# A 5x5 convolution by pairs of rows with shared products, laid into a selective scan

## The chip, the cores and the metric

The kernel runs on one core of a Trainium2 chip. The core has five engines that work side by side: TensorE (PE in the profile, with its weight loads listed as PEld), VectorE (DVE), ScalarE (ACT), GpSimd (POOL) and the queue of SyncE (SP), which here issues the transfers. Each engine takes its instructions strictly in the order of its queue. The metric is the time of one execution in microseconds of device time, the median of several runs. All data are 32-bit floats.

## The reference, cut to what matters

The input x is 4 images of 128 channels and 64 x 64 points. Four layers follow each other, each of the form x = x + f(group_norm(x)) with 32 groups:

```
layer 0: full self-attention over the 4096 points
layer 1: 5x5 convolution, 128 -> 128 channels, padding 2; its taps are
         built from two small tables, an index table and an identity
layer 2: 1x1 projection, split into 2 x 64 channels, the second half
         reversed in time; per half a 4-tap convolution, SiLU, softplus,
         then a selective scan with 64 states per channel over 4096 steps
         (h = exp(delta*A) h + delta*x*B, y = C h + D x); 1x1 projection back
layer 3: 3x3 convolution with bias (the offsets it also computes do not
         reach the output: where(m > 0.01, out, out))
```

The change concerns layer 1:

```
xp = pad(gn(x), 2)
y[o, r, c] = sum over channels i and taps (dy, dx) of
             w[o, i, dy, dx] * xp[i, r + dy, c + dx]
```

## The kernel before, in words

The 128 channels lie on the 128 partitions; an image is 4096 columns. A product on PE is a 128 x 128 weight times 512 columns, accumulated into one PSUM bank (512 floats per partition).

The scan of layer 2 is the backbone. `scan_core` cuts it into ticks: 4 images x 4 chunks of 1024 steps x 2 directions x 16 groups of states x 2 groups of channels, 256 ticks to an image and 1024 in all. In a tick ACT makes the decays exp(delta*A) (`decay`, L801), POOL the drives delta*x*B (`drive`, L808, one 128 x 1024 multiplication), DVE the recurrence itself (`recur`, L818) and the multiplication by C (L821). In some ticks POOL takes that multiplication (`weigh`, L839): two of five for images 0 to 2, one of three for image 3. PE adds up over the states (`collect`, L853). Drives are written two ticks ahead of the recurrence into three buffers; loads of the rows go out four ticks ahead.

Everything else is written as generators that yield after each small step the time that the step is thought to take on PE (PRODUCT = 0.86 us for one 512-column product, HOP and SLOT for other steps). `images` chains them: for each image attention (L405 and L417), the 5x5 convolution (`conv`, L571, closing in `add`, L954 and L955), and the preparation of the scan (`scan_prep`, `scan_operands`), and after those of all four images the back part of images 0 to 2 (projection back, 3x3 convolution). The main loop at the end of `program` interleaves them with the scan: each tick gives a credit of PACE, in two halves, and steps of the other work are written out until the credit is used up. The order on every queue is fixed that way when the program is built; at run time nothing but semaphores decides. If half of the next image's preparation is not written when the scan of one image ends, the loop writes all of it at once (`before`). During the scan of image 3 the credit is ENDPACE.

So image 0's attention, convolution and the first half of its preparation run before any scan. Those of images 1 to 3 run between the ticks of images 0 to 2, and the back parts of images 0 to 2 between the ticks of image 3; the back part of image 3 comes last.

The convolution before: `conv` copies the normalised image into a padded buffer of 68 x 68 in four pieces (ACT, L311), and for each block of 8 rows runs 25 products, one per tap, into one of three banks. After the third product of the next block DVE adds the finished bank to x (L954) and takes the statistics of the sum for the next norm (L955).

Buffers of size: `A0` and `A1` hold a padded or plain image in turn, `V` attention's values, then the normalised input of the scan preparation, and later the padded image of the 3x3 convolution. The 25 taps `cw` are built by DVE during attention of image 0; the 9 taps of the 3x3 convolution `m3` have a buffer of their own, loaded at the start.

Of the kernel before, what the change touches and what calls it, by code (L numbers as in the profile page):

```python
# [24 lines left out]
F32 = mybir.dt.float32  # L25
I32 = mybir.dt.int32
AF = mybir.ActivationFunctionType
ALU = mybir.AluOpType
# [4 lines left out]
P = 128  # L33
GROUPS = 32
GN_EPS = 1e-5
CH = 1024
MM = 512
HALF = P // 2
PAD = 2
# [3 lines left out]

PRODUCT, HOP, SLOT, PACE, ENDPACE, AHEAD = 0.86, 1.7, 0.7, 2.9, 1.5, 4


BQ, BK, BX, BP, CONVB, BD, DSKIP, MAINB, CONVW, ALOG = 0, 1, 2, 3, 4, 5, 6, 7, 8, 12
# [3 lines left out]
def conv_preact_kernel(  # L53
# [16 lines left out]
    nc = tc.nc  # L70
    B, C, H, W = x.shape
    L = H * W
# [4 lines left out]
    NTAP = xhat.shape[1]  # L77
    HP, WP = H + 2 * PAD, W + 2 * PAD
# [8 lines left out]
    const = ctx.enter_context(tc.tile_pool(name="const", bufs=1))  # L87
    small = ctx.enter_context(tc.tile_pool(name="small", bufs=2))
    dram = ctx.enter_context(tc.tile_pool(name="dram", bufs=2, space=DRAM))
    ps = ctx.enter_context(tc.tile_pool(name="ps", bufs=1, space=PSUM))  # L90
    pools, ready = {}, set()

    def bank(tag, name):
        return pools.get(tag, ps).tile([P, MM], F32, tag=tag, name=name)
# [12 lines left out]
    nc.scalar.dma_start(wback[:, 0, :], mats[:, 4, :])  # L107
    nc.scalar.dma_start(wback[:HALF, 1, :], mats[HALF:, 4, :])
    nc.scalar.dma_start(wback[HALF:, 1, :], mats[:HALF, 4, :])
    m3 = const.tile([P, main_w.shape[1], C], F32, name="m3")  # L110
    nc.scalar.dma_start(m3, main_w)

    ident = const.tile([P, P], F32, name="ident")
    make_identity(nc, ident)
# [18 lines left out]
    for d in range(2):  # L133
        r = slice(d * HALF, (d + 1) * HALF)
# [74 lines left out]
    nc.vector.tensor_scalar(hbias, cbias, 0.5, None, ALU.mult)  # L209


    cw = const.tile([P, NTAP, C], F32, name="cw")

    def build_conv_weights(tmp):
        xx_sb = tmp.tile([P, NTAP, C], F32, name="xx_sb")
        nc.sync.dma_start(xx_sb, xhat)
        id_sb = tmp.tile([P, C], F32, name="id_sb")
        nc.sync.dma_start(id_sb, identity)
        picked = tmp.tile([P, 2, NTAP, C // 2], F32, name="picked")
        for n, (which, table, inds) in enumerate((("xx", wxx, indsxx), ("id", wid, indsid))):  # L220
            nr, oc = table.shape[1], table.shape[2]
            acc = picked[:, n]
            one = cw.rearrange("p k c -> p (k c)")[:, : NTAP * oc]
            one = one.rearrange("p (k o) -> p k o", o=oc)
            tab = tmp.tile([P, nr, oc], F32, name=f"tab{which}")
            nc.sync.dma_start(tab, table)
            ii = tmp.tile([P, NTAP], I32, name=f"ii{which}")
            nc.sync.dma_start(ii, inds.to_broadcast([P, NTAP]))
            fi = tmp.tile([P, NTAP], F32, name=f"fi{which}")
            nc.vector.tensor_copy(fi, ii)  # L230

            ng = tmp.tile([P, NTAP], F32, name=f"ng{which}")
            nc.vector.tensor_scalar(ng, fi, 0.0, float(nr), ALU.is_lt, ALU.mult)
            nc.vector.tensor_tensor(fi, fi, ng, ALU.add)
            nc.vector.tensor_scalar(fi, fi, 0.0, float(nr - 1), ALU.max, ALU.min)
            for r in range(nr):
                hit = tmp.tile([P, NTAP], F32, name=f"hit{which}{r}")
                nc.vector.tensor_scalar(hit, fi, float(r), None, ALU.is_equal)
                hit_b = hit.unsqueeze(2).to_broadcast([P, NTAP, oc])
                tab_b = tab[:, r : r + 1, :].to_broadcast([P, NTAP, oc])  # L240
                if r == 0:
                    nc.vector.tensor_tensor(acc, tab_b, hit_b, ALU.mult)
                else:
                    nc.vector.tensor_tensor(one, tab_b, hit_b, ALU.mult)
                    nc.vector.tensor_tensor(acc, acc, one, ALU.add)
                yield HOP

        for t in range(2):
            def every(ap):
                return ap.rearrange("p k (o t) -> p k o t", t=2)[:, :, :, t]  # L250

            idb = id_sb.rearrange("p (o t) -> p o t", t=2)[:, :, t].unsqueeze(1)
            idb = idb.to_broadcast([P, NTAP, C // 2])
            nc.vector.tensor_tensor(every(xx_sb), every(xx_sb), picked[:, 0], ALU.mult)
            nc.vector.tensor_tensor(every(cw), picked[:, 1], idb, ALU.mult)
            yield HOP
        nc.vector.tensor_tensor(cw, cw, xx_sb, ALU.add)

    ASIZE, VSIZE = (H + 4) * (W + 4), (H + 2) * (W + 2)

    def large(n, name):
        return pools["big"].tile([P, ASIZE], F32, tag=f"A{n % 2}", name=name)
# [6 lines left out]
    def stats_tile(name):  # L272
        return small.tile([P, NM, 6], F32, tag=f"gn_st{name[0]}", name=f"st_{name}")
# [36 lines left out]
    def normalise(dst, src, gn):  # L310
        nc.scalar.activation(dst, src, AF.Identity, scale=gn[0], bias=gn[1])  # L311
# [230 lines left out]
    def conv(b, xs, tag, st, weights, k, finish, name, residual=False):  # L542

        pad = k // 2
        hp, wp = H + 2 * pad, W + 2 * pad
        size = VSIZE if tag == "V" else ASIZE
        xp = pools["big"].tile([P, size], F32, tag=tag, name=f"xp{name}_{b}")
        xp = xp[:, : hp * wp].rearrange("p (h w) -> p h w", w=wp)
        nc.gpsimd.memset(xp[:, :pad, :], 0.0)
        nc.gpsimd.memset(xp[:, hp - pad :, :], 0.0)  # L550
        nc.gpsimd.memset(xp[:, pad : hp - pad, :pad], 0.0)
        nc.gpsimd.memset(xp[:, pad : hp - pad, wp - pad :], 0.0)
        gn = yield from group_norm(st, f"{name}{b}")
        xh = xs.rearrange("p (h w) -> p h w", w=W)

        def piece(i):
            h0, h1 = i * H // 4, (i + 1) * H // 4
            normalise(xp[:, pad + h0 : pad + h1, pad : pad + W], xh[:, h0:h1, :], gn)

        piece(0)  # L560
        yield HOP / 2
        piece(1)
        done = None
        for i in range(NM):
            if i < 2:
                piece(2 + i)
            acc = bank("saz"[i % 3], f"pc{name}_{b}_{i}")
            for t in range(k * k):
                dy, dx = divmod(t, k)
                y = i * RPM + dy  # L570
                nc.tensor.matmul(  # L571
                    acc.rearrange("p (r w) -> p r w", w=W), weights[:, t, :],
                    xp[:, y : y + RPM, dx : dx + W],
                    start=t == 0, stop=t == k * k - 1 and not residual,
                )
                if t == 2 and done is not None:
                    finish(*done)
                if t % 3 == 2:
                    yield 3 * PRODUCT
            if residual:  # L580
                nc.tensor.matmul(acc, ident, xs[:, bass.ts(i, MM)], start=False, stop=True)
            yield PRODUCT
            done = i, acc
        yield HOP
        finish(*done)

# [334 lines left out]
    def program(safe):  # L923
        mats4, ynds, ends = {}, {}, {}
        ready.clear()

        def load(tile, b):
            for c in range(NCH):
                nc.sync.dma_start(tile[:, bass.ts(c, CH)], xf[b][:, bass.ts(c, CH)])
                yield 0.0  # L930
# [13 lines left out]
        def front(b, xn, v):  # L944

            xs = large(b + 1, f"xs_{b}")[:, :L]
            yield from load(xs, b)
            st = stats_tile(f"e{b}")
            yield from attention(b, xs, xn, v, st, safe)
            st2 = stats_tile(f"s{b}")  # L950

            def add(i, acc):
                cut = bass.ts(i, MM)
                nc.vector.tensor_tensor(xs[:, cut], acc, xs[:, cut], ALU.add)  # L954
                nc.vector.bn_stats(st2[:, i, :], xs[:, cut])  # L955

            yield from conv(b, xs, f"A{b % 2}", st, cw, 5, add, "e")

            def mat(name):
                return dram.tile([NCH, P, CH], F32, tag=name, name=f"{name}_{b}")  # L960

            mats4[b] = (
                [mat("bm"), mat("cm")], mat("dd"), mat("dxd"), mat("xcd"),
                dram.tile([P, L], F32, tag="xsd", bufs=B, name=f"xsd_{b}"),
            )
            ynds[b] = dram.tile([NM, P, MM], F32, tag="ynd", bufs=B, name=f"ynd_{b}")
            operands = yield from scan_prep(b, xs, st2, mats4[b])
            if b + 1 < B:
                return (yield from both(operands, start(b + 1, 10)))
            yield from operands  # L970
# [52 lines left out]
        inner, last = range(PER, NM - PER), range(NM - PER, NM)  # L1023
# [15 lines left out]
        with ExitStack() as es, tc.manual_schedule():  # L1039
# [60 lines left out]
            for _ in chain(end(B - 1, range(PER)), back(B - 1)):  # L1100
                pass

    program(False)


# [11 lines left out]
    with tc.If(again > 0):  # L1117
        program(True)
# [59 lines left out]
```

## Time and profile before

| what | value |
|---|---|
| time, median of 3 runs | 4684.2 us (4680.8 to 4685.3) |
| profiled span | 4679.2 us |
| PE busy | 4151.4 us, 89% |
| DVE busy | 3764.6 us, 80% |
| POOL busy | 3522.0 us, 75% |
| ACT busy | 2313.3 us, 49% |
| 5x5 convolution on PE (L571 into pce) | 1600 records, two to a product |
| scan on DVE, multiplications L821 and recurrences L818 | one or two of each to a tick |

The page shows the share of busy time of each engine, the span in 40 slices, and groups of instructions by line. A record of PE is half a product of the program, and its listed length includes the time it overlaps with its neighbours, so the count of records and their spacing say more than their mean. Shares over the whole span mix three stages with different limits; they have to be read from windows.

### The profile page before, as it was taken

How to read it: one execution, taken by the hardware profiler on the slowest of the kernel's cores; microseconds unless marked ns; L12 is line 12 of the kernel's file. 1: busy time of each engine (PE TensorE's matmuls, PEld its weight loads, DVE VectorE, ACT ScalarE, POOL GpSimd, SP SyncE). 2: the span in 40 equal slices, each digit the busy share in tenths (PEclk: the TensorE clock that was granted, in tenths of full speed). 3: DMA queues.
4: the chain of work that ended last, by engine and by line, in shares of the span. 5: the costliest groups of instructions: out<-in, count | busy, mean ns of one | idle time of the engine just before them, and what ended most of it. 6: DMA issues, size and time to landing. Idle time of an engine off the chain costs nothing. (4 is left out here: it accounts for less than half of the span.)

```text
span 4679.2 us, 43928 instructions
## 1 busy us (share of the span) xinstructions
PE 4151.4 (89%) x13840; PEld 1538.3 (33%) x13840; DVE 3764.6 (80%) x3673; ACT 2313.3 (49%) x4166; POOL 3522.0 (75%) x1644
## 2 busy tenths in 40 slices
PE   6999997999999988999999979999999748576767
PEld 3444443333333323333333323333333202121212
DVE  7222104999999998999999999899989899999993
ACT  2333205666665356666654466666543644444431
POOL 2333202898888978898989869888889689999992
PEclk9999998999999999999999989999999968787878
DMA  1000005544444555445444564454445565656561
GB/s 65 0 0 1 0 5 184 186 168 163 163 169 150 178 203 214 155 164 175 169 158 164 187 227 169 157 177 164 168 147 177 201 224 199 229 193 229 186 230 46
DMA packets 210434, 718.90 MB, mean 154 GB/s; under 512 B 24848, under 2 KB 25744, under 8 KB 210064
## 3 DMA queue, kind: packets, MB, share of 16 engines
q1 hardware_dynamic: 208448, 714.69, 43.7%
q8 instruction: 111, 1.82, 0.2%
q10 hardware_dynamic: 1744, 1.32, 0.1%
q14 instruction: 131, 1.07, 0.1%
HBM read 649.07 MB, written 66.85 MB: 153 GB/s over the span
## 5 line engine op out<-in xcount | busy, mean ns | idle before, releaser
L808 POOL TENSOR_TENSOR db<-dx,br 128x1024 f32<-128x1024 f32 x1024 | 2404.4, 2367 | 377.8 <-DVE hc L818 94.8
L801 ACT ACTIVATE da<-de,a_neg 128x512 f32<-128x512 f32 (+1 forms) x1795 | 1343.9, 752 | 926.9 <-DVE da L818 600.3
L405 PE MATMUL sc<-r,x 128*128 128x512 f32 x2048 | 1087.5, 613 | 44.0 <-ACT last L834 16.4
L417 PE MATMUL acc<-pt,v 128*128 128x512 f32 x2048 | 1049.1, 594 | 1.5
L839 POOL TENSOR_TENSOR hc<-hc,cr 128x1024 f32<-128x1024 f32 x392 | 928.5, 2369 | 19.0 <-ACT last L834 15.5
L411 ACT ACTIVATE pt<-sc 128x512 f32<-128x512 f32 x1024 | 604.0, 590 | 613.4 <-PE sc L405 577.8
L821 DVE TENSOR_TENSOR hc<-da,cr 128x512 f32<-128x512 f32 (+1 forms) x1095 | 847.1, 774 | 71.7 <-DVE da L818 0.9
L853 PE MATMUL y<-hc,sel 128*32 128x512 f32 x4096 | 654.0, 653 | 272.7 <-POOL hc L839 247.5
L818 DVE TENSOR_TENSOR_SCAN da<-da,last,db 128x512 f32<-128x512 f32 (+1 forms) x474 | 740.5, 1562 | 16.2 <-POOL db L808 8.9
L571 PE MATMUL pce<-xpe,cw 128*128 128x512 f32 x1600 | 724.6, 606 | 24.8 <-ACT xpe L311 17.8
L818 DVE TENSOR_TENSOR_SCAN da<-da,da,db 128x512 f32<-128x512 f32 x463 | 595.8, 1287 | 26.2 <-ACT da L801 25.8
L405 PEld LDWEIGHTS sc<-r,x 128*128 128x128 f32 x2048 | 358.9, 190 | 642.7 <-issue 385.9
L417 PEld LDWEIGHTS acc<-pt,v 128*128 128x128 f32 x2048 | 388.4, 190 | 498.9 <-issue 480.0
L571 PEld LDWEIGHTS pce<-xpe,cw 128*128 128x128 f32 x1600 | 297.3, 190 | 452.4 <-issue 424.0
L818 DVE TENSOR_TENSOR_SCAN hc<-da,last,db 128x512 f32<-128x512 f32 (+1 forms) x294 | 442.7, 1506 | 2.9 <-POOL db L808 1.2
L818 DVE TENSOR_TENSOR_SCAN hc<-da,hc,db 128x512 f32<-128x512 f32 x308 | 395.1, 1283 | 45.1 <-ACT da L801 15.6
L459 POOL TENSOR_TENSOR sidep<-sidep,pt 128x512 f32<-128x512 f32 x120 | 161.3, 1344 | 307.0 <-ACT pt L411 307.0
L853 PEld LDWEIGHTS y<-hc,sel 128*32 128x32 f32 x4096 | 93.5, 111 | 728.7 <-POOL hc L839 333.2
L571 PE MATMUL pcm<-xpm,m 128*128 128x512 f32 x576 | 287.5, 647 | 31.4 <-ACT xpm L311 31.4
L459 DVE TENSOR_TENSOR sided<-sided,pt 128x512 f32<-128x512 f32 x120 | 90.3, 753 | 249.7 <-ACT pt L411 248.4
L818 DVE TENSOR_TENSOR_SCAN da<-da,db 128x512 f32<-128x512 f32 (+1 forms) x158 | 235.7, 1492 | 17.0 <-ACT da L801 9.3
L834 ACT COPY last<-da 128x1 f32<-128x1 f32 x473 | 74.0, 156 | 270.1 <-DVE hc L821 268.2
(167 smaller groups left out, 2251.9 us busy)
## 6 DMA issues: line engine op xcount, KB each, us to landing
br<-bm SPq DMA_DIRECT2D x512, 512.0 KB, 5.0
cr<-cm SPq DMA_DIRECT2D x512, 512.0 KB, 3.9
de<-dd SPq DMA_DIRECT2D x64, 512.0 KB, 4.6
dx<-dxd SPq DMA_DIRECT2D x64, 512.0 KB, 6.2
x<-in_x_dram SPq DMA_DIRECT2D x16, 512.0 KB, 5.7
xs<-in_x_dram SPq DMA_DIRECT2D x16, 512.0 KB, 6.8
xsd<-xs SPq DMA_DIRECT2D x16, 512.0 KB, 5.1
xcd<-xc SPq DMA_DIRECT2D x16, 512.0 KB, 2.7
```

Of the source, the lines that this page charges most:

```text
L405: nc.tensor.matmul(sc, xn[:, bass.ts(j, P)], rq[blk], start=True, stop=True)
L411: nc.scalar.activation(pt, sc, AF.Exp)
L417: nc.tensor.matmul(acc[blk], v[:, j, :], ring[:, u % NRING, :], start=j == 0, stop=j == NJT - 1)
L459: eng.tensor_tensor(s, s, ring[:, u % NRING, :], ALU.add)
L571: nc.tensor.matmul(acc.rearrange("p (r w) -> p r w", w=W), weights[:, t, :], xp[:, y : y + RPM, dx : dx + W], start=t == 0, stop=t == k * ...
L801: nc.scalar.activation(da, rep["de", b, c, d, g][:, bass.ts(h, size)], AF.Exp, scale=a_neg[:, at(i)])
L808: nc.gpsimd.tensor_tensor(dbs[i], rep["dx", b, c, d, g], rows["b", b, c, d, q], ALU.mult)
L818: nc.vector.tensor_tensor_scan(h, da, db[:, cut], before, ALU.mult, ALU.add)
L821: nc.vector.tensor_tensor(hc[:, cut], h, rows["c", b, c, d, q][:, cut], ALU.mult)
L834: nc.scalar.copy(last[b][:, at(i)], end)
L839: nc.gpsimd.tensor_tensor(hcs[i], hcs[i], rows["c", b, c, d, q], ALU.mult)
L853: nc.tensor.matmul(y[r : r + SG, :], sel, hcs[i - KG + 1 + gg][:, bass.ts(h, MM)], start=q == 0, stop=False, tile_position=(0, r), skip_gr ...
```

## The change

Two vertically adjacent output rows share work. With x0 to x5 the six padded input rows that they see and w0 to w4 the five rows of taps (each standing for its five horizontal taps):

```
q  = (w1 + w2) x2 + (w3 + w4) x4
y0 = q + w0 x0 + w1 (x1 - x2) + w3 (x3 - x4)
y1 = q + w0 x1 + w2 (x3 - x2) + w4 (x5 - x4)
```

This takes 2 + 3 + 3 rows of taps to two rows of output in place of 5 + 5. The new `conv_pairs` works on chunks of 16 rows: one bank for q (8 rows of pairs), one for the even and one for the odd rows, 512 columns each.

- The sums of taps w1 + w2 and w3 + w4 are made once by DVE (two additions of 128 x 640) behind the 25 taps.
- The differences of neighbouring rows are made by POOL into a buffer `diffs` in `V`: per image eight subtractions of 8 or 9 rows of 66 columns, each behind the normalised piece it reads.
- ACT copies q from its bank to SBUF. In image 0 POOL adds the copy to x, once for even and once for odd rows. In the later images (`lean`) PE adds it to the banks of the even and odd rows by a product with the identity.
- DVE adds the finished banks to x with a row stride and takes the statistics after the odd rows.
- The padded buffer has rows of 66 columns; a row's right padding is the next row's left padding.
- `m3` now lies in the first nine taps of `cw`. The 3x3 taps are loaded when the last image's 5x5 convolution has been written; a copy of the 5x5 taps is kept in device memory for a second pass that runs only if attention's sums fall out of range.
- PACE goes from 2.9 to 2.8.

The core of the diff:

```diff
-PRODUCT, HOP, SLOT, PACE, ENDPACE, AHEAD = 0.86, 1.7, 0.7, 2.9, 1.5, 4
+PRODUCT, HOP, SLOT, PACE, ENDPACE, AHEAD = 0.86, 1.7, 0.7, 2.8, 1.5, 4
...
-    m3 = const.tile([P, main_w.shape[1], C], F32, name="m3")
-    nc.scalar.dma_start(m3, main_w)
...
+    m3 = cw[:, : main_w.shape[1], :]
...
+        for n in range(2):
+            row = cw[:, (1 + 2 * n) * 5 :]
+            nc.vector.tensor_tensor(
+                cw[:, NTAP + n * 5 : NTAP + (n + 1) * 5, :], row[:, :5], row[:, 5:10], ALU.add
+            )
+        nc.sync.dma_start(kept, m3)
...
+        def odd(j, n):
+            nc.gpsimd.tensor_tensor(
+                diffs[:, j * WQ : (j + n) * WQ].rearrange("p (h w) -> p h w", w=WQ),
+                rows[:, 2 * j + 1 : 2 * (j + n) : 2, :], rows[:, 2 * j + 2 : 2 * (j + n) + 1 : 2, :],
+                ALU.subtract,
+            )
...
+        for c in range(L // CH):
+            j = c * CK
+            if c < 2:
+                piece(2 + c)
+            if c < 3:
+                differences(c + 1)
+            accs = [
+                (bank("s", f"pq_{b}_{c}"), ((SUM12, image, 2 * j + 2), (SUM34, image, 2 * j + 4))),
+                (bank("a", f"pe0_{b}_{c}"),
+                 ((0, image, 2 * j), (1, diff, j), (3, diff, j + 1))),
+                (bank("z", f"pe1_{b}_{c}"),
+                 ((0, image, 2 * j + 1), (2, diff, NP + j + 1), (4, diff, NP + j + 2))),
+            ]
+            for n, (acc, parts) in enumerate(accs):
+                k, total = 0, len(parts) * K5
+                for w, view, r in parts:
+                    for dx in range(K5):
+                        k += 1
+                        nc.tensor.matmul(
+                            flat(acc), cw[:, w * K5 + dx, :], view(r, dx),
+                            start=k == 1, stop=k == total and (n == 0 or not lean),
+                        )
+                        if k == 3 and done is not None:
+                            done()
+                            done = None
+                        if k % 3 == 0:
+                            yield 3 * PRODUCT
+                if n == 0:
+                    qs = pools["bg"].tile([P, MM], F32, tag="w", bufs=4, name=f"q_{b}_{c}")
+
+                    def done(acc=acc, qs=qs, c=c):
+                        nc.scalar.copy(qs, acc)
+                        for y in range(0 if lean else 2):
+                            nc.gpsimd.tensor_tensor(
+                                chunk(xs, c, y), chunk(xs, c, y), flat(qs), ALU.add
+                            )
+                    yield PRODUCT
+                else:
+                    if lean:
+                        nc.tensor.matmul(acc, ident, qs, start=False, stop=True)
+                        yield PRODUCT
+
+                    def done(acc=acc, c=c, y=n - 1):
+                        add(c, y, acc)
...
-            yield from conv(b, xs, f"A{b % 2}", st, cw, 5, add, "e")
+            yield from conv_pairs(b, xs, f"A{b % 2}", st, st2, b > 0 or safe)
+            if b + 1 == B:
+                nc.sync.dma_start(m3, main_w)
```

More of the change, by code (lines that the diff above doesn't have):

```diff
@@ L209, in conv_preact_kernel @@
     nc.vector.tensor_scalar(hbias, cbias, 0.5, None, ALU.mult)
-    cw = const.tile([P, NTAP, C], F32, name="cw")
+    SUM12, SUM34 = 5, 6
+    cw = const.tile([P, NTAP + 10, C], F32, name="cw")
+    taps5 = cw[:, :NTAP, :]
+    m3 = cw[:, : main_w.shape[1], :]
+    kept = dram.tile([P, main_w.shape[1], C], F32, tag="kept", bufs=1, name="kept")
     def build_conv_weights(tmp):
@@ L249, in every @@
             def every(ap):
-                return ap.rearrange("p k (o t) -> p k o t", t=2)[:, :, :, t]
+                return ap.rearrange("p k (o t) -> p k o t", t=2)[:, :NTAP, :, t]
             idb = id_sb.rearrange("p (o t) -> p o t", t=2)[:, :, t].unsqueeze(1)
@@ L256, in build_conv_weights @@
             yield HOP
-        nc.vector.tensor_tensor(cw, cw, xx_sb, ALU.add)
-    ASIZE, VSIZE = (H + 4) * (W + 4), (H + 2) * (W + 2)
+        nc.vector.tensor_tensor(taps5, taps5, xx_sb, ALU.add)
+        for n in range(2):
[4 more added lines that the diff above has]
+        nc.sync.dma_start(kept, m3)
+    ASIZE, VSIZE = HP * (W + PAD) + PAD, (H + 2) * (W + 2) + PAD
     def large(n, name):
@@ L585, in conv, with conv_pairs, piece, even @@
         finish(*done)
+    def conv_pairs(b, xs, tag, st, st2, lean):
+        NP, CK = H // 2, CH // W // 2
+        WQ = W + PAD
+        xp = large(b, f"xpe_{b}")
+        rows = xp[:, : HP * WQ].rearrange("p (h w) -> p h w", w=WQ)
+        xh = xs.rearrange("p (h w) -> p h w", w=W)
+        nc.gpsimd.memset(rows[:, :PAD, :], 0.0)
+        nc.gpsimd.memset(xp[:, (HP - PAD) * WQ : HP * WQ + PAD], 0.0)
+        nc.gpsimd.memset(rows[:, PAD : HP - PAD, :PAD], 0.0)
+        gn = yield from group_norm(st, f"e{b}")
+        diffs = pools["big"].tile([P, VSIZE], F32, tag="V", name=f"df_{b}")
+        nc.gpsimd.memset(diffs[:, 2 * (NP + 1) * WQ :], 0.0)
+        def piece(i):
+            h0, h1 = i * H // 4, (i + 1) * H // 4
+            normalise(rows[:, PAD + h0 : PAD + h1, PAD:], xh[:, h0:h1, :], gn)
+        def odd(j, n):
[4 more added lines that the diff above has]
+            )
+        def even(j, n):
+            at = (NP + j) * WQ
+            nc.gpsimd.tensor_tensor(
+                diffs[:, at : at + n * WQ].rearrange("p (h w) -> p h w", w=WQ),
+                rows[:, 2 * j + 1 : 2 * (j + n) : 2, :], rows[:, 2 * j : 2 * (j + n) - 1 : 2, :],
+                ALU.subtract,
+            )
+        def differences(i):
+            last = i == 3
+            odd(8 * i, 8 + last)
+            even(8 * i + 1, 8 + last)
+        def by_rows(t, n):
+            return [t[:, o : o + n * WQ].rearrange("p (h w) -> p h w", w=WQ) for o in (0, PAD)]
+        padded, differ = by_rows(xp, HP), by_rows(diffs, 2 * (NP + 1))
+        def image(r, dx):
+            late = dx // PAD > 0
+            dx -= late * PAD
+            return padded[late][:, r : r + 2 * CK - 1 : 2, dx : dx + W]
+        def diff(r, dx):
+            late = dx // PAD > 0
+            dx -= late * PAD
+            return differ[late][:, r : r + CK, dx : dx + W]
+        def chunk(t, c, y):
+            v = t[:, bass.ts(c, CH)].rearrange("p (h t w) -> p h t w", t=2, w=W)
+            return v[:, :, y, :]
+        def flat(t):
+            return t.rearrange("p (h w) -> p h w", w=W)
+        piece(0)
+        yield HOP / 2
+        piece(1)
+        differences(0)
+        K5 = 5
+        steps, done = [], None
+        def add(c, y, acc):
+            nc.vector.tensor_tensor(chunk(xs, c, y), flat(acc), chunk(xs, c, y), ALU.add)
+            if y == 1:
+                for i in (2 * c, 2 * c + 1):
+                    nc.vector.bn_stats(st2[:, i, :], xs[:, bass.ts(i, MM)])
+        for c in range(L // CH):
[30 more added lines that the diff above has]
+                        for y in range(0 if lean else 2):
+                            nc.gpsimd.tensor_tensor(
+                                chunk(xs, c, y), chunk(xs, c, y), flat(qs), ALU.add
+                            )
+                    yield PRODUCT
[5 more added lines that the diff above has]
+                        add(c, y, acc)
+        yield HOP
+        done()
@@ L925, in program @@
         ready.clear()
+        if safe:
+            nc.sync.dma_start(m3, kept)
         def load(tile, b):
@@ L950, in front @@
             st2 = stats_tile(f"s{b}")
[L952 to L955, printed above, removed]
-            yield from conv(b, xs, f"A{b % 2}", st, cw, 5, add, "e")
+            yield from conv_pairs(b, xs, f"A{b % 2}", st, st2, b > 0 or safe)
+            if b + 1 == B:
+                nc.sync.dma_start(m3, main_w)
             def mat(name):
```

## The prediction

> **What bounds the kernel now.** I read the slices first, to cut the span into stages.
>
> ```profile
> PE   6999997999999988999999979999999748576767
> ...
> DVE  7222104999999998999999999899989899999993
> ...
> POOL 2333202898888978898989869888889689999992
> PEclk9999998999999999999999989999999968787878
> ```
>
> There are three stages. In slices 1 to 6 TensorE (PE) works almost alone: attention of image 0, then its 5x5 convolution. From slice 7 to 31 PE, VectorE (DVE) and GpSimd (POOL) are all near full: the scan of images 0 to 2 runs there, with attention, convolution and scan preparation of images 1 to 3 laid between its ticks. In the last eight slices (scan of image 3 beside the 3x3 convolutions) PE falls off and DVE stays full. The changed convolution lies in the first two stages.
>
> Then windows, cut at the places where the lines of the convolution begin and end. Columns: window, length, busy time of PE, weight loads, DVE, ACT (ScalarE), POOL, with instruction counts, granted clock, DMA share, GB/s.
>
> ```profile
> 542.00:787.00 245.00, 231.44 (x591) 96.57 (x592) 39.46 (x70) 49.55 (x76) 6.70 (x7) 0.97 0.15 53
> 1024.00:1376.00 352.00, 345.73 (x1312) 126.23 (x1304) 324.17 (x329) 216.00 (x444) 313.84 (x135) 1.00 0.49 167
> 1500.00:1614.00 114.00, 114.00 (x350) 42.42 (x349) 110.28 (x113) 45.88 (x70) 102.12 (x44) 1.00 0.50 173
> 1614.00:1762.00 148.00, 127.65 (x440) 43.59 (x439) 136.46 (x160) 86.68 (x134) 112.69 (x53) 0.96 0.59 207
> 787.00:3737.00 2950.00, 2797.91 (x10113) 1026.38 (x10114) 2704.71 (x2815) 1711.89 (x3262) 2542.62 (x1120) 0.98 0.50 175
> 3900.00:4300.00 400.00, 273.16 (x819) 76.29 (x817) 386.42 (x225) 175.79 (x278) 382.25 (x172) 0.81 0.63 219
> ```
>
> Row 1, image 0's convolution and preparation: POOL 6.7 of 245 us, DVE 39: PE alone sets the time. Row 2, scan with attention: PE 98%, DVE 92%, POOL 89%: PE first, DVE close behind. Row 3, scan with convolution: PE 100%, DVE 97%. Row 4, scan with preparation: DVE 92%, PE 86%. Row 6 shows what DVE reaches when PE isn't in its way: 96.6%, POOL 95.6%.
>
> The waits inside the attention stretch (1030 to 1370 us; total us, times, longest) say how PE holds the scan:
>
> ```profile
> DVE da L818 <- ACT da L801: 6.1, 7, 1.4
> ACT pt L411 <- PE sc L405: 50.3, 54, 3.2
> ACT da L801 <- DVE da L818: 54.7, 30, 5.8
> ```
>
> ACT takes the scores from PE (L411) and the scan's decays (L801) in one queue. When PE is late ACT stands 50 us in all, the next decay is late, and DVE's scan waits for it. So in attention a tick lasts as long as PE's share of it.
>
> The groups that price the work:
>
> ```profile
> L571 PE MATMUL pce<-xpe,cw 128*128 128x512 f32 x1600 | 724.6, 606 | 24.8 <-ACT xpe L311 17.8
> L808 POOL TENSOR_TENSOR db<-dx,br 128x1024 f32<-128x1024 f32 x1024 | 2404.4, 2367 | 377.8 <-DVE hc L818 94.8
> L839 POOL TENSOR_TENSOR hc<-hc,cr 128x1024 f32<-128x1024 f32 x392 | 928.5, 2369 | 19.0 <-ACT last L834 15.5
> L459 POOL TENSOR_TENSOR sidep<-sidep,pt 128x512 f32<-128x512 f32 x120 | 161.3, 1344 | 307.0 <-ACT pt L411 307.0
> ```
>
> One product of the program is two records: 4 images x 8 blocks x 25 taps = 800 products, 1600 records.
>
> **What the Trainium skill says.** "Perfetto Trace Analysis", section Identifying the Most-Contended Engine: matmul busy time is a poor measure because matmuls overlap. The trace agrees: records average 606 ns, but in image 0's convolution 200 products went from 542.3 to about 716.5 us, 0.87 us each, 0.43 a record. "FP8 and Floating Point Precision", section TensorE Precision Notes, gives fp32 four passes; "TensorE: Matmul & The Clock Gate", section Back-to-back issue gap, 518 cycles at 2.4 GHz for 512 columns; four make 0.863 us (an estimate from the two), as traced. "GPSIMD Engine Reference", section 3.1 (Elementwise — side-by-side cycle accounting), has 4497 ns for an fp32 addition of 2048 elements, 2.2 ns each; here 2367/1024 = 2.31. Its section 8 (Key points) warns of contention with VectorE for SBUF; the addition L954 took 691 ns with POOL idle (image 0) and 677 ns beside the scan, so I charge none.
>
> **The change, part by part.**
>
> *Products.* A chunk of 16 rows took 2 x 25 = 50 products; now 10 for the shared sum, 15 each for even and odd rows: 40. An image: 200 to 160. Images 1 to 3 add 8 identity products that put the shared sum into PSUM: 168.
>
> *Image 0 (alone on PE).* 40 x 0.87 = 34.8 us less. Added: POOL's 8 subtractions and 8 additions of the shared sum, some 1.3 us each, on an idle engine; the first pair is wanted after 15 products (13 us) and ready about 5 us after the start; later pairs have 34 us. The ACT copy (0.59 us by L465's row) runs beside products. At the end two statistics follow the last addition instead of one: +0.7 us. Net -34.
>
> *Images 1 to 3 on PE.* 32 x 0.864 = 27.6 us less each, 83 us in all. That is a pool of PE time, not yet a gain; the pace turns it into time. PACE 2.9 to 2.8 gives each tick 0.1 us less of PE work. In the built order of both kernels, counting ticks by the scan's y products, attention takes 182 ticks instead of 176, the convolution 52 instead of 60 (its estimate falls from 173 to 144.5 us), preparation is issued at the same place (tick 240 to 252 of 256). So no queue of leftover work meets the next image.
>
> *A tick with attention.* 3.63 us now (mean of 12 stretches of 32 ticks between the L808 records), of which the scan's own y products take about 0.55 on PE (16 groups of 1.06 us to 32 ticks). The rest, 3.08, scales by 2.8/2.9: -0.106. If PE still set it: 3.53. DVE's floor: 324.17 busy in 352 us is 3.35 a tick, at row 6's 96.6% 3.46. Two engines both this near their limit disturb each other, so I take 3.54; 3.46 (DVE alone) and 3.63 (no gain) are the ends.
>
> *A tick with the convolution.* 3.59 now (the three stretches of 32 ticks inside it). PE falls to about 3.47, but DVE has the same additions and statistics (16 x 0.69 = 11 us) in 52 ticks instead of 60, +0.03: DVE's 110.28/114 x 3.56 + 0.03 = 3.47, at 96.6% 3.60. POOL: 1.4 operations of 2.37 a tick are 3.31; the subtractions (6 of 528, 2 of 594 elements) take 1.22 us each at 2.31 ns, 1.39 at L459's rate; I take 1.35, 11 us in 52 ticks, +0.21: 3.52. I take 3.62, DVE and POOL together.
>
> *Sum for an image.* Before 144 x 3.63 + 60 x 3.59 = 738; after 150 x 3.54 + 52 x 3.62 = 719, plus 2 more ticks in the preparation at DVE's bare 3.4 = 7: 726; early attention (32 ticks near 4.0) -0.05 each: -2. That is -14; three images -41.
>
> *New waits.* A subtraction stands in POOL's queue behind nothing but ahead of the drives L808 (two ticks ahead, three buffers), and waits for ACT's normalised piece (1.23 us). Four such waits per image, each up to a tick while POOL is ahead of ACT; 5 us of lead cover most. Between 0 and 10 us an image; I take 1, so +3. ACT's copy of the shared sum waits for a product three products old, as DVE's addition does now (L954: 9 us in all from 1000 to 3500 us); ACT is 60% busy: nothing. The buffer of the differences is the one preparation zeroes next, so that memset waits for the last product; the norm behind it waits for the same convolution anyway (4.3 us, L305): nothing. The load of the 3x3 weights moves from the start into one wait on the DMA queue at image 3; loads run four ticks ahead: nothing, and about 2 us less at the start.
>
> Total: 4684 - 34 - 41 + 3 - 2 = 4610.
>
> **Rivals.**
> A. PE stays the bound everywhere, and its 83 us come out whole: 4684 - 36 - 83 = 4565. For: PE 98 to 100% in rows 2 and 3. Against: DVE at 92 and 97%.
> B. DVE and POOL take over at once: the pace moves idle time about, ticks stay, only image 0 gains: 4684 - 34 = 4650. For: DVE's total is unchanged and row 3 is nearly full; against: in attention DVE idles 8%.
> C. Slower: POOL's strided subtractions cost double (21 us an image) and each of the four waits holds the drives 5 us; the convolution's 52 ticks give 52 x (3.62 - 3.31) = 16 us back: (21 + 20 - 16) x 3 = +75, with PE's saving in the ticks unused: 4684 - 34 + 75 = 4725. For: POOL at 89% has the least lead, in a strict queue. Against: its slack in preparation (row 4: 76%) and that all its waits in attention are short.
>
> **How the numbers follow.** Forecast 0.58, A 0.14, B 0.21, C 0.07. The range reaches from just below A to B: 4562 to 4652; C and the far ends of A and B are left out. Faster 0.90, same 0.03 (between B and C), slower 0.07.
>
> **What would show it.** Image 0's convolution should start to end in about 139 us of products instead of 174. The stretch from the first drive to the start of image 3's scan should shrink from 2950 to about 2912 us. In attention PE's share should fall to 96 to 97% and DVE's rise to about 94 to 95%; in the convolution POOL should rise to 95% or more. The last image's 942 us should not move. Wrong would be: subtractions far above 1.4 us, DVE waiting for db from POOL in the convolution, or ticks in attention still at 3.6.

## The result, and the profile after

The changed kernel takes 4616.9 us (median of 4 runs, 4615.9 to 4618.7) against 4684.1 (4680.8 to 4685.3): ratio 0.9858, 95% interval 0.9841 to 0.9875. That is 67 us less; the forecast was 4610, 74 less.

The slices of the profile after:

```profile
PE   6999998999999978999999979999999658585767
...
DVE  7222115989998989999999989999999999999993
...
POOL 2333304889988968898989869899899699999992
PEclk9999998999999989999999989999999878787878
```

The picture is the same; POOL has filled up in places. Windows of the profile after, in the columns used before (window, length, busy time of PE, weight loads, DVE, ACT, POOL, clock, DMA): attention, convolution, the scans of images 0 to 2, the scan of image 3.

```profile
1024.00:1340.00 316.00, 308.62 (x1174) 112.51 (x1167) 298.07 (x304) 196.22 (x401) 287.89 (x124) 1.00 0.49 168
1476.00:1577.00 101.00, 100.98 (x311) 37.22 (x313) 96.29 (x99) 41.23 (x60) 96.71 (x44) 1.00 0.49 169
755.00:3693.00 2938.00, 2740.60 (x9925) 999.46 (x9923) 2716.44 (x2828) 1724.49 (x3284) 2573.30 (x1146) 0.97 0.51 177
3890.00:4290.00 400.00, 257.05 (x768) 70.67 (x772) 385.27 (x238) 178.37 (x280) 376.52 (x175) 0.78 0.60 211
```

In attention PE is at 97.7% (98.2 before) and DVE at 94.3% (92.1). In the convolution POOL has risen from 90 to 95.8%, DVE is at 95% (97), PE still at 100%. The preparation is best compared over the same ticks. Ticks 224 to 256 of image 0, before and after:

```profile
1620.27:1772.89 152.62, 129.67 (x458) 45.80 (x456) 140.73 (x167) 93.52 (x146) 114.70 (x55) 0.96 0.60 210
```

```profile
1584.20:1742.49 158.29, 125.27 (x444) 45.70 (x444) 144.17 (x168) 95.94 (x150) 110.07 (x53) 0.91 0.53 193
```

PE falls from 85 to 79%. Over images 0 to 2, PE is idle for 32 us more in the scan than before, and 24 us of that lie in these last 32 ticks of each image. The granted clock is lower there too, in all three images: 0.91, 0.90 and 0.87 against 0.96, 0.92 and 0.91. Whether that is a cause or a consequence of the idle time isn't settled.

In the waits of the attention stretch (1030 to 1340 us) ACT stands less for the scores and so DVE less for the decays:

```profile
DVE da L956 <- ACT da L939: 1.6, 2, 1.0
```

```profile
ACT da L939 <- DVE da L956: 57.2, 40, 5.7
ACT pt L421 <- PE sc L415: 26.4, 26, 2.7
```

6.1 us of waiting for decays is now 1.6, and 50.3 us of waiting for scores 26.4 (in 310 us instead of 340). DVE's named waits are small in both kernels, so they alone don't show what sets the tick; the runs below do more for that.

What the new instructions cost (line, engine, form, count, busy us, mean ns, idle before):

```profile
L717 PE MATMUL pe<-q,ident 128*128 128x512 f32 x48 | 25.5, 614 | 0.0
L630 POOL TENSOR_TENSOR df<-xpe 128x528 f32<-128x528 f32 x12 | 13.5, 1127 | 0.0
L622 POOL TENSOR_TENSOR df<-xpe 128x528 f32<-128x528 f32 x12 | 13.3, 1106 | 1.3 <-ACT xpe L321 1.3
L709 ACT COPY q<-pq 128x512 f32<-128x512 f32 x16 | 9.3, 581 | 112.9 <-PE pq L696 112.9
```

A subtraction of 528 elements takes 1.11 to 1.13 us where I had charged 1.35, and all of them together waited 1.3 us for ACT. Of the 112.9 us before the copies 109.4 are image 0's, where ACT has nothing else to do.

The end of image 0's convolution, from the timeline of DVE (start, length, what, idle before), before and after:

```profile
717.51 0.69 DVE L954 TENSOR_TENSOR xs<-pce,xs 128x512 f32<-128x512 f32 x1 [20.12 <-PE pce L571]
```

```profile
683.78 0.69 DVE L673 TENSOR_TENSOR xs<-pe,xs 128x512 f32<-128x512 f32 x1 [12.23 <-PE pe L696]
684.50 1.29 DVE L676 BATCH_NORM_STATS2 st_s<-xs 128x6 f32<-128x512 f32 x2
```

The last addition starts at 683.8 instead of 717.5 us.

**Where the time went.** The drives on POOL, by which I meant to cut the span, run ahead of the scan by an amount that changes (at the start of image 3's scan 18.7 us before, 3.8 us after); counted by them the stage lasts 2938 us against 2951. So I count by DVE's recurrences (the first one of each tick), in us of the profiled runs:

| stretch | before | after | difference |
|---|---|---|---|
| to the first recurrence | 789.2 | 754.9 | -34.3 |
| 768 ticks of images 0 to 2 | 2967.0 | 2938.6 | -28.4 |
| from there to the end | 923.0 | 919.9 | -3.1 |
| span | 4679.2 | 4613.4 | -65.8 |

And inside an image, mean us per tick over images 0 to 2:

| ticks | what runs beside them | before | after |
|---|---|---|---|
| 0-32 | rest of preparation, attention begins | 3.998 | 3.904 |
| 32-160 | attention | 3.659 | 3.569 |
| 160-192 | change from attention to convolution | 3.812 | 3.870 |
| 192-224 | convolution | 3.580 | 3.585 |
| 224-256 | its end, preparation | 4.880 | 4.974 |

These means hide something. By image the 256 ticks moved by +3.9, +1.5 and -33.9 us. The attention ticks alone moved by -8.1, -9.4 and -17.1 us; in images 0 and 1 the rest of the image takes all of that back. A table by image stands below, with the runs on the pace.

### The profile page after: what moved, and what is told of

Read it like the earlier page. It is cut to its first block, busy times and chain, and to the rows that moved or that the text cites. A ratio compares the mean times of both kernels' runs of the same rounds, so it can differ in the third digit from the quotient of the medians.

```text
span 4613.4 us, 43452 instructions
## 1 busy us (share of the span) xinstructions
PE 4058.3 (88%) x13568; PEld 1496.7 (32%) x13568; DVE 3758.6 (81%) x3672; ACT 2320.9 (50%) x4180; POOL 3561.4 (77%) x1684
## 5 line engine op out<-in xcount | busy, mean ns | idle before, releaser
L946 POOL TENSOR_TENSOR db<-dx,br 128x1024 f32<-128x1024 f32 x1024 | 2403.9, 2367 | 339.0 <-DVE hc L956 75.7
L991 PE MATMUL y<-hc,sel 128*32 128x512 f32 x4096 | 674.1, 654 | 279.6 <-POOL hc L977 262.5
L581 PE MATMUL pcm<-xpm,cw 128*128 128x512 f32 x576 | 289.8, 651 | 31.7 <-ACT xpm L321 31.7
L696 PE MATMUL pe<-df,cw 128*128 128x512 f32 x640 | 289.3, 597 | 0.0
L449 PE MATMUL zp<-pt,ones 128*32 128x512 f32 x1536 | 208.9, 595 | 0.0
```

The costliest lines, as they stand in the source:

```text
L581: nc.tensor.matmul(acc.rearrange("p (r w) -> p r w", w=W), weights[:, t, :], xp[:, y : y + RPM, dx : dx + W], start=t == 0, stop=t == k * ...
L696: nc.tensor.matmul(flat(acc), cw[:, w * K5 + dx, :], view(r, dx), start=k == 1, stop=k == total and (n == 0 or not lean),)
L946: nc.gpsimd.tensor_tensor(dbs[i], rep["dx", b, c, d, g], rows["b", b, c, d, q], ALU.mult)
L991: nc.tensor.matmul(y[r : r + SG, :], sel, hcs[i - KG + 1 + gg][:, bass.ts(h, MM)], start=q == 0, stop=False, tile_position=(0, r), skip_gr ...
```

## The experiments

Times of the kernel before beside these runs were 4685 to 4689 us, so ratios are compared. "Stage" is the 768 ticks of images 0 to 2 as above, from the one trace of each run.

**Image 0 alone.** `conv_pairs` for image 0, the old `conv` for the others, pace 2.9. The core of the edit (the old addition and the larger padded buffer come back with it):

```diff
...
+            if b == 0:
+                yield from conv_pairs(b, xs, f"A{b % 2}", st, st2, safe)
+            else:
+                yield from conv(b, xs, f"A{b % 2}", st, cw, 5, add, "e")
```

> Only image 0 uses the pairs of rows; images 1 to 3 keep the 25-tap convolution, pace back at 2.9. Theory (image 0 is alone on TensorE, the later images gain through the pace): 4684 - 34 = 4650, first recurrence about 34 us earlier than before, the 768 ticks of images 0 to 2 within 5 us of the 2967 us of before. Rival (the whole gain hangs on TensorE's total, or the moved weight load matters): below 4640 or above 4660.

Measured: 4657.2 us, ratio 0.9930 (0.9913 to 0.9947), 32 us less. First recurrence at 757.4, stage 2971.6, attention ticks 3.658. So about half of the gain is image 0's, where PE works alone, and it is worth its products and no more. The later images are those of the kernel before, and their stage differs from it by 4.6 us: a difference of that size isn't taken for an effect here.

**The pace undone.**

```diff
-PRODUCT, HOP, SLOT, PACE, ENDPACE, AHEAD = 0.86, 1.7, 0.7, 2.8, 1.5, 4
+PRODUCT, HOP, SLOT, PACE, ENDPACE, AHEAD = 0.86, 1.7, 0.7, 2.9, 1.5, 4
```

> The changed kernel with the pace back at 2.9. Theory (an attention tick lasts as long as TensorE's share of it): attention ticks back to 3.65 us from 3.57, the other work done about 9 ticks before the image ends, these bare at about 3.4; per image +7, in all about 4638. Rival (VectorE and GpSimd set the ticks, the pace only moves idle time): attention ticks stay at 3.57, 4617.

Measured: 4647.7 us, ratio 0.9909 (0.9892 to 0.9926). Attention ticks 3.643, stage 2972.2. With fewer products but the old pace the later images gain nothing: each tick carries as much other work as before, and the work is only done sooner. I had expected the end of each image to run bare, which is not what happened. The preparation beside image 0 starts at tick 232 instead of 242, the attention after it at tick 250, and in image 2 the back part of image 0 follows from tick 744 on. The cost, 34 us of stage against the changed kernel, is more than the 7 us an image that I had expected.

**The pace alone, on the kernel before.**

```diff
-PRODUCT, HOP, SLOT, PACE, ENDPACE, AHEAD = 0.86, 1.7, 0.7, 2.9, 1.5, 4
+PRODUCT, HOP, SLOT, PACE, ENDPACE, AHEAD = 0.86, 1.7, 0.7, 2.8, 1.5, 4
```

> The kernel before with only the pace at 2.8. Theory (a smaller share of TensorE work shortens attention ticks, and the saved products are what makes room for it): attention ticks 3.57 instead of 3.66, about -13 us an image, but some 25 us of other work are left at each image's end and cost about that: ratio 0.998 to 1.005. Rival (the pace is the whole gain of the later images, with the products irrelevant): 0.993, as much as images 1 to 3 gained.

Measured: 4704.0 us, ratio 1.0036 (1.0023 to 1.0048), slower. Attention ticks fall to 3.566, as in the changed kernel, but ticks 224 to 256 take 5.295 instead of 4.880: what didn't fit is written out at the image's end. The four stages together:

| stage, us | pace 2.9 | pace 2.8 |
|---|---|---|
| 25 taps in images 1 to 3 | 2967.0 | 2983.8 |
| pairs of rows in images 1 to 3 | 2972.2 | 2938.6 |

Neither edit gains in the scan without the other: the saved products pay only with the lower pace, and the lower pace only with the products gone. The same four by image, us for its 256 ticks:

| kernel | image 0 | image 1 | image 2 |
|---|---|---|---|
| 25 taps, pace 2.9 | 983.7 | 981.9 | 1001.5 |
| 25 taps, pace 2.8 | 997.7 | 993.3 | 992.8 |
| pairs of rows, pace 2.9 | 997.2 | 993.0 | 982.0 |
| pairs of rows, pace 2.8 | 987.6 | 983.4 | 967.6 |

With pace 2.8 in both, the saved products are worth 10, 10 and 25 us. Against the kernel before, though, the whole 28 us come from image 2, whose scan takes 18 us longer there than the other two. It does so again in two other runs with the 25 taps in images 1 to 3 at pace 2.9 (image 0 alone, and three of seven below), so it isn't chance; why it does, and why it no longer does after the change, stays open.

**The pace lower still.** PACE 2.7.

> The changed kernel with the pace at 2.7: 0.1 us less TensorE work to a tick again, but some 25 us of it are left when an image's scan ends and are written out at once. Theory (VectorE is next behind TensorE): attention ticks fall only to about 3.50 (-11 us an image) and the leftover costs about 20 an image: about 4640. Rival (TensorE alone): attention ticks 3.46 and the whole near 4635 as well, told apart by the tick. Rival (VectorE and GpSimd already set the ticks): ticks stay at 3.57 and the whole is near 4677.

Measured: 4629.8 us, ratio 0.9873 (0.9856 to 0.9890). Attention ticks 3.521: not the 3.46 of PE alone and not the unchanged 3.57, so something besides PE's share holds part of the 0.1 us. The stage is 2938.3, the same as with 2.8; ticks 192 to 224 are at 3.859 and 224 to 256 at 5.264. What attention gains up to tick 192, the end of the image gives back. What comes after the stage is 14 us longer than in the changed kernel. The leftover cost less than I had expected (4640).

**Subtractions doubled**, and **left out**, in images 1 to 3. Doubled:

```diff
-            odd(8 * i, 8 + last)
-            even(8 * i + 1, 8 + last)
+            for _ in range(2 if b > 0 else 1):
+                odd(8 * i, 8 + last)
+                even(8 * i + 1, 8 + last)
```

> In images 1 to 3 each subtraction of neighbouring rows is run twice, with the same result: GpSimd has 9 us more per image, all in the convolution. Theory (GpSimd is near its limit in the convolution but can catch up in the preparation): about +4 per image, 4629. If GpSimd isn't the bound at all: 4617. If it is the full bound there: +27, 4644.

Left out, with the products reading rows of the image:

```diff
-            odd(8 * i, 8 + last)
-            even(8 * i + 1, 8 + last)
+            if b == 0:
+                odd(8 * i, 8 + last)
+                even(8 * i + 1, 8 + last)
...
-                 ((0, image, 2 * j), (1, diff, j), (3, diff, j + 1))),
+                 ((0, image, 2 * j), (1, first, 2 * j + 1), (3, first, 2 * j + 3))),
...
-                 ((0, image, 2 * j + 1), (2, diff, NP + j + 1), (4, diff, NP + j + 2))),
+                 ((0, image, 2 * j + 1), (2, second, 2 * j + 3), (4, second, 2 * j + 5))),
```

(`first` and `second` read the differences in image 0 and the padded image in the others, so this kernel leaves the subtractions out of the layer and computes something else with as many products.)

> Images 1 to 3 leave the subtractions of neighbouring rows out; the same number of products reads rows of the padded image instead, so the output isn't the reference's. Theory (the 9 us of subtractions cost about 60% of themselves, as their doubling did): -5 to -6 us an image, ratio about 0.982, the gain at the start of the convolution. Rival (the first set hides and only the second one costs): no change, 0.9858.

Measured: doubled 4636.9 us, 0.9890 (0.9872 to 0.9907), stage 2955.8; left out 4616.0 us, 0.9848 (0.9832 to 0.9865), stage 2938.2, the same as with them. My expectation from the doubling, that the first set costs like the second, was wrong. DVE's waits for drives over the stage (755 to 3693 us), first left out, then as changed, then doubled, show it:

```profile
DVE da L963 <- POOL db L953: 2.0, 5, 0.5
```

```profile
DVE da L956 <- POOL db L946: 12.5, 17, 1.8
```

```profile
DVE da L957 <- POOL db L947: 26.5, 22, 5.7
```

The first set adds 10 us of these waits and nothing to the stage; only about half of the 10 us lies in ticks 160 to 224, where the subtractions are. The second set adds 14, and the stage 17. Of those 17 us 15 lie in ticks 160 to 192, where each convolution starts with four subtractions in a row, or eight when they are doubled. The timeline of the doubled run shows the last of the eight in image 0's scan, the drives behind it and the recurrence that needs the first of them:

```profile
1463.02 1.12 POOL L630 TENSOR_TENSOR df<-xpe 128x528 f32<-128x528 f32 x1
1464.09 4.67 POOL L947 TENSOR_TENSOR db<-dx,br 128x1024 f32<-128x1024 f32 x2
1466.48 1.29 DVE L957 TENSOR_TENSOR_SCAN da<-da,last,db 128x512 f32<-128x512 f32 x1 [4.51 <-POOL db L947]
```

The other two images have one such wait each, of 5.6 and 5.7 us. Eight subtractions take 8.6 us (1455.5 to 1464.1), four 4.3. Drives run two ticks ahead, some 7 us at 3.57 a tick (an estimate), less what POOL is behind. So four stay inside this lead and eight don't. It is the length of the row that counts here and not POOL's total load: the run with three of seven below puts 47 us more on POOL, and its stage is shorter.

**The shared sum added on GpSimd in every image.**

```diff
-            yield from conv_pairs(b, xs, f"A{b % 2}", st, st2, b > 0 or safe)
+            yield from conv_pairs(b, xs, f"A{b % 2}", st, st2, safe)
```

> All images add the shared sum on GpSimd, as image 0 does, instead of the identity products: TensorE has 6.9 us less per image in images 1 to 3, GpSimd 10 us more. Theory (in the convolution GpSimd, at 96% of it, is nearer the limit than TensorE): +5 to +8 us an image as with the doubled subtractions, ratio to the kernel before about 0.990. Rival (TensorE sets the time there): -7 us an image, ratio about 0.981.

Measured: 4632.9 us, 0.9881 (0.9864 to 0.9898), stage 2949.4, +11. At this pace the 8 identity products (6.9 us of PE an image) are the cheaper place, even though PE is full; the additions take 10 us of POOL. The size was less than expected (+15 to +24). The comparison isn't an even one: the pace stayed at 2.8, and the runs above show that saved products bring nothing until the pace is lowered. Additions on GpSimd with a lower pace were not tried.

**Relief for VectorE**, on the changed kernel and on the kernel before: in the scans of images 0 to 2 GpSimd takes three of seven multiplications by C instead of two of five.

```diff
-            return i % 5 in (1, 3) if ticks[i][0] + 1 < B else i % 3 == 2
+            return i % 7 in (1, 3, 5) if ticks[i][0] + 1 < B else i % 3 == 2
```

> The changed kernel with GpSimd taking three multiplications of seven instead of two of five in the scans of images 0 to 2: GpSimd +0.07 us a tick, VectorE about -0.04. If VectorE is the next bound behind TensorE in attention: attention ticks 3.53 from 3.57 and up to -20 us in all. If GpSimd is: +10 to +50 us, most of it in the convolution. If TensorE still is: attention ticks unchanged.

> The kernel before with GpSimd taking three multiplications of seven instead of two of five. If relief of VectorE pays only where VectorE sets the time (preparation and convolution), as in the changed kernel: attention ticks stay at 3.66, 7 us less per image, ratio about 0.995. If TensorE sets the time throughout the kernel before: 1.000.

Measured: on the changed kernel 4593.8 us, 0.9800 (0.9783 to 0.9817), stage 2917.8, 21 less than without it. On the kernel before 4684.5 us, 0.9995 (0.9986 to 1.0004), stage 2966.4: nothing. Windows of the kernel before with this edit (attention, convolution):

```profile
1024.00:1376.00 352.00, 346.13 (x1310) 127.05 (x1308) 322.58 (x324) 217.18 (x447) 321.90 (x140) 1.00 0.49 170
1500.00:1614.00 114.00, 114.00 (x350) 42.31 (x349) 108.55 (x109) 45.10 (x68) 102.82 (x45) 1.00 0.49 173
```

PE stays at 98 and 100% and the stage is as long as before; DVE's relief is idle time. The changed kernel with it (stage):

```profile
755.00:3673.00 2918.00, 2732.74 (x9925) 997.14 (x9923) 2684.59 (x2785) 1724.85 (x3284) 2620.30 (x1168) 0.97 0.51 178
```

DVE has 32 us less work (2684.6 against 2716.4), and the stage is 21 us shorter, by 5 to 8 us in each image. Attention ticks moved little (3.557 from 3.569), the convolution's to 3.546 from 3.585, ticks 224 to 256 to 4.823 from 4.974. So VectorE had become a bound, and the relief shows at the end of the image more than in attention, where I had put it. This kernel beats both.

**Three attempts to go on from there.** GpSimd taking two of three in the last 24 ticks of each image:

```diff
+            if ticks[i][0] + 1 == B:
+                return i % 3 == 2
+            return i % 3 > 0 if i % TICKS >= 232 else i % 7 in (1, 3, 5)
```

> Three of seven as in the run before it, and two of three in the last 24 ticks of each scan of images 0 to 2, where the preparation lies: VectorE 7 us less per image there, GpSimd 13 us more. If VectorE's load sets the time of the preparation: 4 to 6 us less per image than with three of seven, ratio 0.976 to 0.978. If its chain of waits does: no change, 0.980. If GpSimd becomes the bound: above 0.980.

Measured: 4606.2 us, 0.9826 (0.9810 to 0.9843), 12 us longer than three of seven alone, but only 1.6 us of that in the stage (2919.4); ticks 224 to 256 at 4.838, no better than 4.823. More relief of VectorE in the preparation does nothing; its chain of waits or GpSimd holds it by then, and which one isn't settled.

The convolution's steps counted cheaper and the pace at 2.75, first on the changed kernel:

```diff
-                            yield 3 * PRODUCT
+                            yield 2.8 * PRODUCT
```

> The changed kernel with the pace at 2.75 and the convolution's steps counted at 14/15 of their time, so that attention gives each tick less TensorE work and the convolution, where TensorE isn't the bound, more; the work ends within 2 ticks of where it did. Theory (VectorE's floor under attention is near): attention ticks 3.545, -3 us an image, convolution unchanged: ratio about 0.984. Rival (every engine is at its limit everywhere in the scan): no change, 0.986.

Measured: 4614.0 us, 0.9845 (0.9829 to 0.9862), no difference from the changed kernel that the intervals show. Its stage is 2917.1, 21 less, with attention ticks at 3.551; but the first recurrence came 3 us later, the first 32 ticks of image 3 took 8 us more and the rest 5 more. The 8 us are in part work moved, not saved: the last preparation ends at tick 772 instead of 764, so in image 3's scan. Counted to tick 800 this run gains 14 us. A rest 4 to 8 us longer and a first recurrence 2 to 4 us later show in several other runs of this study too; why is open. Then both together:

> Both edits together: three of seven on GpSimd, pace 2.75 with the convolution's steps counted at 14/15. If TensorE is again the bound under attention once VectorE is relieved: attention ticks 3.50 to 3.52 instead of 3.557, 5 us less per image, ratio about 0.977. If GpSimd (3.38 us of multiplications a tick) or the chains set it by now: no change, 0.980.

Measured: 4591.8 us, 0.9796 (0.9773 to 0.9819), stage 2899.3, attention ticks 3.536, above the 3.50 to 3.52 expected. The two gains nearly add up in the scan: counted to tick 800, 20 us for three of seven, 14 for the pace and 31 for both. That is 61 us below the kernel before (3016.2 against 3077.0), of 83 us of saved products. At the end of the run it can't be told from three of seven alone.

## Why the prediction was right, point by point

- *What bounds.* PE was said to set the ticks of the kernel before. Moving multiplications from DVE to POOL changes nothing there (0.9995), while PE is at 98 to 100%. A lower pace shortens attention ticks from 3.66 to 3.57; that fits, but it doesn't single PE out, since it takes attention's work on ACT, DVE and POOL from the tick too.
- *Image 0, -34.* -34.3. The 16 operations on POOL and the 4 copies lay beside PE as said. The 2 us at the start, from the moved weight load, did not come: image 0's convolution begins at 543.3 us against 542.3.
- *A tick with attention, -0.09.* -0.090 (3.659 to 3.569) in the mean, but -0.063, -0.073 and -0.134 by image. That the mean falls on the forecast is partly luck. That something stands close behind PE is borne out by pace 2.7 (3.521); that it is DVE's load is not: relief of DVE moved the attention ticks by 0.012 only.
- *A tick with the convolution, +0.03.* +0.005. Subtractions are 1.11 us and not 1.35, and their waits were 1.3 us in all for four images where I had allowed 0 to 10 an image. No cost of theirs shows in the stage (2938.2 without them). POOL is at 95.8%, as expected.
- *The sum for the later images, -38.* -28.4. Attention's 128 steady ticks give -11.5 an image in the mean, as the rate says. I let the rate also hold in the last 22 ticks of attention, but ticks 160 to 192, with the change from attention to convolution, lose 1.9 us an image. What DVE waits for there has changed: more for the closing products of attention (9.5 us in the three images, from 3.9) and for decays (4.1, from 1.4), no longer for the convolution's products (0, from 7.0). Why the change-over lengthened isn't shown; leaving the subtractions out does not mend it (3.860 against 3.870). Ticks 224 to 288, where the early ticks were to give -2, are nearly unchanged in the mean, but go +8.2, -8.6 and -3.6 us by image. So the forecast was near in its size, while its picture of three like images, each 13 us shorter, does not hold.
- *New waits.* ACT's copies waited 3.4 us in all in images 1 to 3, and the last image and the end moved by -3.1 us, so neither the copies nor the moved weight load show.
- *What was to show it.* Image 0's convolution takes 140.5 us to its last addition instead of 175.2, as said (139, 174). The stage counted by drives was to shrink by 38 us and shrank by 13, for the reason given above. In attention PE is at 97.7%, a little over the 96 to 97 expected.
- *Rivals.* A (all 83 us of PE come out) failed, in part at least because DVE became a bound; with DVE relieved and the pace at 2.75 (the last run) 61 come out by tick 800. B (DVE and POOL take over, the ticks stay, only image 0 gains) failed as well: the ticks fell. The run with pace 2.9 comes near its number, 0.9909 or 4641 where B said 4650, but with the pace left as it was. C (POOL's queue) was no danger with one set of subtractions; a second set cost 17 us.
- *Two readings beside the point.* L954 reads one of its operands from PSUM, so its times don't test the contention that the Trainium skill, "GPSIMD Engine Reference", section 8 (Key points), names for VectorE instructions with two inputs from SBUF. And the Trainium skill, "Perfetto Trace Analysis", section Identifying the Most-Contended Engine, says that pipelined instructions look smaller in the trace; here a record (606 ns) is longer than its spacing (0.43 us).

## What to carry to other kernels

When two engines are both within a few per cent of the limit, relief of either alone may show nothing: here the relief of VectorE was worth 0 before the products were saved and 21 us in the stage after. In this kernel, whose order is written out by a pace, saved work turned into time only when the pace was lowered by about as much as was saved, and the lower pace alone cost 17 us of stage. Work added to a strict queue is free as long as a row of it fits into the lead of what stands behind it: four subtractions in a row did, eight did not. And look at each repetition, not at the mean alone: three images that were thought alike moved by +4, +2 and -34 us.

## What the runs showed of the hardware that was not expected

GpSimd's subtraction of strided rows (66 columns out of every second row) took 1106 ns for 528 elements, 2.1 ns each, less than its multiplication of contiguous rows (2367 ns for 1024, 2.3 each). Its addition of the copied sum to every second row of x (L711) took 1265 ns for 512, 2.5 each, so what makes the difference isn't settled. The strided addition on DVE (8 rows out of every second one, L673) took 678 ns against 681 for the contiguous one (L954).
